# Two-layer gated network: the first layer's fourth batch in seven block products

## The chip, the cores and the metric

The kernel runs on one core of a Trainium2 chip. The core has a matrix engine (TensorE, PE in the profile), a vector engine (VectorE, DVE), a scalar engine (ScalarE, ACT), GpSimd (POOL), and SyncE (SP), which here only issues transfers. They run side by side, each through its own instructions in order, and wait for each other by semaphores. Matrix products are written to PSUM, everything else lies in SBUF, and DRAM is reached by DMA. The metric is the device time of one execution in microseconds, lower is better.

## The reference, cut to what matters

Two layers over x of shape (4, 512, 256). Each layer normalizes, computes a mixer `s` and a gate `g`, and adds their product to x. The gate is a feed-forward block with hidden width 1024, a Hadamard transform (`fwht`) of the hidden values and a down projection.

```python
def ffn(x, W1, W2, W3):
    hidden = silu(x @ W1.T) * (x @ W3.T)      # 256 -> 1024
    return fwht(hidden) @ W2.T                # 1024 -> 256

x = L0_attn_x
xn = layernorm(x)
s = L0_attn(xn)              # reduces to xn + rmsnorm(xn @ M) * norm_w
x = x + s * silu(ffn(xn, L0_ffn_W1, L0_ffn_W2, L0_ffn_W3))
xn = layernorm(x)
s = L1_attn(xn)              # causal attention with its own norm
x = x + s * silu(ffn(xn, L1_ffn_W1, L1_ffn_W2, L1_ffn_W3))
```

## The kernel before

Rows are tiled by 128. A batch has 512 rows (`NT` = 4 tiles of 128), the model width 256 is two blocks of 128, the hidden width 1024 eight blocks (`NH`). Each batch passes layer 0 first, all four of them (`f0_0` to `f0_3`; the profile leaves digits of names out, so `f_3gu` is the gate/up product of batch 3), then layer 1 (`f1_0` to `f1_3`).

**Numbers in two parts.** A value that enters a product is kept as a rounded part and the rest (`split`, L59: a cast on ScalarE, then a subtraction on VectorE). A product of two such values is three matmuls: high by high, high by low, low by high (`mm3`, L80).

**W2.** The Hadamard transform is moved into W2: `prep_w2` (L139) takes three steps of sums and differences on VectorE and a product with a 128 x 128 Hadamard matrix on TensorE, for each layer once. Layer 1's W2 is prepared beside batch 1 of layer 0 and stays in SBUF (`w2_tile`, L173, four buffers of 8 KB per partition under one tag).

**Layer 0** (`ffn`, L467). For each hidden block c, two gate/up products of 512 columns (six matmuls each), SiLU on ScalarE, multiplication on VectorE, a split, and the down product of the block before (twelve matmuls of 256 columns). All other work is given to a `Beside` object (L878) as a list of generators with a number of steps each; `slot` (L897) advances them evenly, twice per block. So program order is written by the slots, and from it a scheduler that simulates the engines makes the order of instructions of every engine. In `Beside` lie the gate of the batch before (`gate`, L691), the mixer (L714), the norm and transposition of the batch after (`norm`, L432), and preparations of weights.

**Layer 1** (`ffn_s`, L562). Here, for each quarter q of the hidden width, x (transposed) and the gate and up weights are each cut into 2 x 2 blocks, and their product is formed by Winograd's variant of Strassen's scheme from seven block products instead of eight. Each is six matmuls of 256 columns (`product`, L621). It needs sums of the weight blocks (`A11 ... S4`) and of x's blocks (`B11 ... T4`), and copies and additions between PSUM banks. There TensorE's order is fixed by hand (`line["fixed"]`): after each product, `place(n)` runs what the list `beside[q][n]` names. An integer there is a down product of the quarter before, a tuple one of an earlier quarter.

`prep_s` (L322) makes one quarter's weight sums: it loads four blocks (`sraw`, 512 KB), forms four sums on VectorE (`ssum`), splits the seven blocks (384 KB and 512 KB at a time) by a negated rounded copy and a rounded copy on ScalarE (`sp`), an accumulating transfer issued by GpSimd, which subtracts the rounded part, and stores both parts in DRAM. It is a generator of five steps. `load_s` (L350) brings a quarter back, two parts of 896 KB (`sw`), into two of four buffers, which the weights of layer 0 (`split_w13`, L118) hold before. The four quarters are prepared once, beside batches 2 and 3 of layer 0, and loaded again for every batch of layer 1.

`t_blocks` (L358) finds room for x's blocks: in W2's buffers for odd batches, in those of transposed xn (`xt_pair`, L304, two buffers) for even ones, and for batch 0 half of it in general scratch (`t4`, ten buffers of 4 KB per partition).

**Attention of layer 1.** `Attention` (L737): `xt` and `scaled` make the transposed, normalized and scaled input from the transposes `xt_half` (L744); `tq` and `v` are its first products. For batch 0 the transposes lie in `Beside` of `f0_3`, `tq` at the tail of `f0_3`, and `v` in the first quarter of `f1_0`.

Of the kernel before, what the change touches and what calls it, by code (L numbers as in the profile page):

```python
# [23 lines left out]
B = 4  # L24
# [11 lines left out]
def kernel(ctx: ExitStack, tc: tile.TileContext, a: dict, out: bass.AP):  # L36
# [101 lines left out]

    def prep_w2(layer, raws, dst, scratch):  # L139
# [3 lines left out]
        w2h, w2l = dst  # L143
        for half in range(2):
# [12 lines left out]
            if not native:  # L157
                bh = t4(f"w2bh_{layer}_{half}", [P, NH, P], F32R)
                bl = t4(f"w2bl_{layer}_{half}", [P, NH, P], F32R)
                split(cur, bh, bl)  # L160
                yield
# [11 lines left out]
    def w2_tile(name):  # L173
        return wp.tile([P, NH, D], F32R, tag="w2", name=name, bufs=4)

    def w2_tiles(layer):
        return w2_tile(f"w2h_{layer}"), w2_tile(f"w2l_{layer}")

# [125 lines left out]
    def xt_pair(name):  # L304

        both = act.tile([P, 2, 2, S], F32R, tag="xt", name=name, bufs=2)
        return both[:, 0], both[:, 1]
# [9 lines left out]

    A11, A12, A22, S1, S2, S3, S4 = range(7)
    B11, B22, B21, T1, T2, T3, T4 = range(7)
    sdram = {}  # L320

    def prep_s(q):  # L322

        raw = t4(f"sraw{q}", [P, 4, D])
        nc.sync.dma_start(raw, a["w13_1"][q])
        yield
        sums = t4(f"ssum{q}", [P, 4, D])
# [7 lines left out]
        sdram[q] = there = [  # L335
            dram.tile([P, 7, D], F32, tag=f"s{i}", name=f"s{i}_{q}", bufs=4) for i in range(2)
        ]

        for at, n, src in ((0, 3, raw), (3, 4, sums)):
            src = src[:, :n, :]  # L340
            hi, neg = (t4(f"sp{at}_{i}_{q}", [P, n, D], F32R) for i in range(2))
# [8 lines left out]
    def load_s(q, n):  # L350
        parts = [
            wp.tile([P, 7, D], F32R, tag="w13", name=f"sw{i}_{n}_{q}", bufs=4) for i in range(2)
        ]
        for i in range(2):
            nc.sync.dma_start(parts[i].bitcast(F32), sdram[q][i])
        return parts

    def t_blocks(b):  # L358

        if b % 2:  # L360
            whole = [w2_tile(f"tb{i}_{b}") for i in range(2)]
        else:
            whole = [
                act.tile([P, NH, D], F32R, tag="xt", name=f"tb{i}_{b}", bufs=2)
                for i in range(2 if b else 1)
            ]
        parts = [[w[:, i, :] for i in range(7)] for w in whole]
        if len(parts) < 2:
            lo3, lo4 = t4(f"tb3_{b}", [P, 3, D], F32R), t4(f"tb4_{b}", [P, 4, D], F32R)
            whole = [whole[0], None]  # L370
            parts.append([lo3[:, i, :] for i in range(3)] + [lo4[:, i, :] for i in range(4)])
            return parts, [(whole[0][:, 0, :], lo3[:, 0, :]),
                           (whole[0][:, 1:3, :], lo3[:, 1:3, :]),
                           (whole[0][:, 3:7, :], lo4)]
        return parts, [
            tuple(w[:, 0, :] for w in whole),
            tuple(w[:, 1:3, :] for w in whole),
            tuple(w[:, 3:7, :] for w in whole),
        ]

# [51 lines left out]
    def norm(layer, b):  # L432
# [5 lines left out]
        if layer:  # L438
# [18 lines left out]
            return  # L457
        hi, lo = xTs[0, b] = xt_pair(f"xt0_{b}")
# [8 lines left out]
    def ffn(name, xT, w13, w2, slot, defer=1, spare=(), parts=1, behind=False, tail=()):  # L467
# [86 lines left out]
        line["fixed"] = bool(tail)  # L554
        line["last"] = last_up
        for what in tail:
            what()
# [4 lines left out]
    def ffn_s(name, b, pairs, w2, beside, before, last=None):  # L562
# [4 lines left out]
        xh, xl = xTs[1, b]  # L567
# [40 lines left out]
        for q in range(NH // 2):  # L608
# [22 lines left out]
            copy = nc.vector.tensor_copy if q == 1 else nc.scalar.copy  # L631
# [45 lines left out]
            if q:  # L677
                left.pop()()
# [35 lines left out]
    def mixer(b):  # L714
# [5 lines left out]
        for i in range(2):  # L720
# [6 lines left out]
            yield  # L727
        nc.vector.tensor_scalar(r, r, 1.0 / D, RMS_EPS, ALU.mult, ALU.add)
# [6 lines left out]
        yield  # L735

    class Attention:  # L737
# [10 lines left out]
        def xt(self):  # L748
            b, mrb = self.b, mrs[self.b]
            xTs[1, b], (tb11, tb2x, tt) = t_blocks(b)  # L750
            self.xg = t4(f"xgh{b}", [P, 2, S], F32R), t4(f"xgl{b}", [P, 2, S], F32R)
            b1, b2 = self.halves
            early, late = slice(0, D), slice(D, S)
# [161 lines left out]
    NORM, MIXER, W2P = 3, 3, 12  # L915
# [80 lines left out]
    for b in range(B):  # L996
# [5 lines left out]
        if b:  # L1002
            tasks.append((call(gate_all, f"g0_{b - 1}", dn, xns[0, b - 1], xs[b - 1]), 1))
        tasks.append((mixer(b), MIXER))
        if b + 1 < B:
            if b:
                load_x(b + 1)
            if b == 2:
                tasks.append((prep_s(0), 5))
            tasks.append((norm(0, b + 1), NORM))  # L1010
        if b == 0:
            early = w2_tile("early0"), w2_tile("early1")
            spare = [
                [early[i][:, 2 * c : 2 * c + 2, :].rearrange("p a d -> p (a d)") for i in range(2)]
                for c in range(NH // 2)
            ]
        if b == 1:
            raw2_1 = load_w2(1)
            w2_1 = w2_tiles(1)
            tasks.append((prep_w2(1, raw2_1, w2_1, t4), W2P))  # L1020
            tasks.append((prep_second(), 5))
        if b == 2:
            tasks += [(prep_s(1), 5), (norm(1, 0), NORM), (prep_s(2), 5)]
        if b == 3:
            atts = [Attention(0)]
            at = atts[0]
            parts = run(at.xt_half, 0), run(at.xt_half, 1), at.xt, at.scaled, at.split_sums
            tasks += [(call(f), 1) for f in parts]
            norms = {1: norm(1, 1)}
            tasks.append((prep_s(3), 5))  # L1030
        bg = Beside(*tasks)
        if b == 0:
# [153 lines left out]
```

## Time and profile before

| | us |
|---|---|
| three runs | 364.04, 365.92, 366.18 |
| median | 365.92 |
| the profiled execution | 363.47 |
| its span in the profile | 361.3 |
| TensorE busy in it | 354.0 |
| VectorE, ScalarE busy | 278.5, 204.1 |

The span runs from the first to the last instruction; some 2.2 us of the profiled execution lie around it. An engine is busy while an instruction of it runs; matmuls overlap, so one shows about 284 ns where the next starts 118 ns later. In the answers by stretch, the numbers in brackets count instructions, the clock is the share of TensorE's full speed that was granted, and the DMA share is the mean over the core's 16 DMA engines.

The transfers that bear on the change, with their count, size and median time from issue to landing:

```profile
sw<-s SPq DMA_DIRECT2D x32, 896.0 KB, 5.1
...
sraw<-in_w SPq DMA_DIRECT2D x4, 512.0 KB, 3.6
s<-sp SPq DMA_DIRECT2D x4, 512.0 KB, 3.8
ssum<-sp POOLq DMA_DIRECT2D x4, 512.0 KB, 6.5
```

Each line is one group of transfers: destination and source, the queue that issues it, how many, how large, and how long until the data were there.

### The profile page before, as it was taken

The page shows a single profiled execution, that of the slowest core. Times are in us where ns is not written, and L with a number is a line of the kernel's source. Part 1 is how long each engine was busy: PE and PEld are TensorE (multiplying, and loading weights), DVE is VectorE, ACT ScalarE, POOL GpSimd, SP SyncE. Part 2 cuts the span into 40 slices and gives each one's busy share as a digit, 9 for nine tenths or more (in the row PEclk, how much of TensorE's full clock was granted, in tenths as well). Part 3 has the DMA queues.
Part 4 walks back from the last instruction along what each step waited for, and adds up shares of the span by engine and source line. Part 5 has one row for each costly group of instructions (what it writes and reads, how often), then busy time and mean ns, then how long its engine had stood idle before and what let it go on. Part 6 is the DMA issues. An engine that isn't in the chain of part 4 may idle for free.

```text
span 361.3 us, 6295 instructions
## 1 busy us (share of the span) xinstructions
PE 354.0 (98%) x2469; PEld 328.2 (91%) x2469; DVE 278.5 (77%) x584; ACT 204.1 (56%) x380; POOL 25.9 (7%) x30
## 2 busy tenths in 40 slices
PE   8999999999999999989999999999999999999995
PEld 6878998888988898868999999999999999999994
DVE  6897868996669835886986957989669897568645
ACT  4665436274494537764467655576655676446443
POOL 1000201100034101111100001100011000000000
PEclk9999999999999999999999999999999999999999
DMA  6935000301149626979356146572553645345401
GB/s 219 354 111 183 3 0 2 116 0 60 58 116 302 196 76 209 256 289 245 121 205 257 34 175 203 201 239 89 203 204 136 218 174 203 133 153 194 191 2 58
DMA packets 17436, 55.92 MB, mean 155 GB/s; under 512 B 1760, under 2 KB 8064, under 8 KB 17408
## 3 DMA queue, kind: packets, MB, share of 16 engines
q1 hardware_dynamic: 15968, 51.60, 39.7%
q0 software_dynamic: 1152, 3.67, 5.4%
q8 instruction: 19, 0.31, 0.3%
q10 hardware_dynamic: 288, 0.26, 0.2%
q14 instruction: 9, 0.07, 0.1%
HBM read 42.40 MB, written 9.45 MB: 144 GB/s over the span
## 4 chain that ended last, share of the span: by engine, by line
PE 78%; DVE 11%; DMA 6%; ACT 3%; issue 1%; POOL 1%; SPq 0%; DVEq 0%; ACTq 0%
PE f_0gu L70 6%; PE f_1gu L70 6%; PE f_2gu L70 6%; PE f_0dn L70 5%; PE f_2dn L70 5%; PE f_1dn L70 5%; PE f_3dn L70 4%; PE pv L70 4%; PE tq L70 3%; DMA sraw<-in_w 3%; PE o L70 2%; PE v L70 2%; DMA ssum<-sp 2%; PE sc L70 2%; PE f_3gu L70 2%; PE warm L70 2%
## 5 line engine op out<-in xcount | busy, mean ns | idle before, releaser
L70 PE MATMUL f_0gu<-xt,w 128*128 128x512 f32 (+1 forms) x108 | 24.8, 382 | 0.0
L70 PE MATMUL f_1gu<-xt,w 128*128 128x512 f32 x96 | 24.8, 395 | 0.0
L70 PE MATMUL f_3gu<-xt,w 128*128 128x512 f32 x96 | 24.7, 397 | 0.1
L70 PE MATMUL f_2gu<-xt,w 128*128 128x512 f32 x96 | 24.7, 395 | 0.0
L70 PEld LDWEIGHTS f_0gu<-xt,w 128*128 128x128 f32 x108 | 18.5, 188 | 4.4 <-issue 0.7
L70 PEld LDWEIGHTS f_3gu<-xt,w 128*128 128x128 f32 x96 | 17.2, 188 | 3.5 <-DVE f_3h L529 0.3
L70 PEld LDWEIGHTS f_2gu<-xt,w 128*128 128x128 f32 x96 | 17.2, 188 | 3.2
L70 PEld LDWEIGHTS f_1gu<-xt,w 128*128 128x128 f32 x96 | 17.1, 188 | 3.2
L61 ACT CAST f_1hh<-f_1h 128x512 fp32r<-128x512 f32 x16 | 10.0, 622 | 16.7 <-DVE f_1h L529 13.6
L70 PE MATMUL f_3dn<-w2h,f_3hh 128*128 128x256 f32 x64 | 17.9, 284 | 1.1 <-ACT f_3hh L61 1.1
L70 PE MATMUL f_1dn<-w2l,f_1hh 128*128 128x256 f32 x64 | 17.8, 282 | 0.0
L70 PE MATMUL f_1dn<-w2h,f_1hh 128*128 128x256 f32 x64 | 17.7, 281 | 0.0
L70 PE MATMUL f_3dn<-w2l,f_3hh 128*128 128x256 f32 x64 | 17.7, 281 | 0.0
L70 PE MATMUL f_2dn<-w2l,f_2hh 128*128 128x256 f32 x64 | 17.7, 281 | 0.0
L70 PE MATMUL f_2dn<-w2h,f_2hh 128*128 128x256 f32 x64 | 17.7, 281 | 0.0
L70 PE MATMUL f_3dn<-w2h,f_3hl 128*128 128x256 f32 x64 | 17.2, 282 | 0.0
L70 PE MATMUL f_1dn<-w2h,f_1hl 128*128 128x256 f32 x64 | 17.1, 282 | 0.0
L61 ACT CAST f_2hh<-f_2h 128x512 fp32r<-128x512 f32 x16 | 9.9, 620 | 12.6 <-DVE f_2h L529 9.5
L70 PE MATMUL f_2dn<-w2h,f_2hl 128*128 128x256 f32 x64 | 16.9, 282 | 0.0
L62 DVE TENSOR_TENSOR f_3hl<-f_3h,f_3hh 128x512 fp32r<-128x512 f32 (+1 forms) x17 | 11.1, 656 | 5.1 <-ACT f_3hh L61 5.0
L61 ACT CAST f_3hh<-f_3h 128x512 fp32r<-128x512 f32 (+1 forms) x17 | 10.0, 593 | 8.3 <-DVE f_3h L529 4.2
L62 DVE TENSOR_TENSOR f_2hl<-f_2h,f_2hh 128x512 fp32r<-128x512 f32 x16 | 10.9, 683 | 4.5 <-ACT f_2hh L61 4.4
(482 smaller groups left out, 1147.9 us busy)
## 6 DMA issues: line engine op xcount, KB each, us to landing
sw<-s SPq DMA_DIRECT2D x32, 896.0 KB, 5.1
w2raw<-in_w SPq DMA_DIRECT2D x4, 512.0 KB, 6.1
sraw<-in_w SPq DMA_DIRECT2D x4, 512.0 KB, 3.6
s<-sp SPq DMA_DIRECT2D x4, 512.0 KB, 3.8
ssum<-sp POOLq DMA_DIRECT2D x4, 512.0 KB, 6.5
s<-ssum SPq DMA_DIRECT2D x4, 512.0 KB, 3.0
mrb<-there SPq DMA_DIRECT2D x4, 512.0 KB, 3.8
w13raw<-in_w SPq DMA_DIRECT2D x3, 512.0 KB, 7.1
```

What stands on the lines that cost most here:

```text
L61: h = nc.scalar.copy(hi, src)
L62: return h, engine.tensor_tensor(lo, src, hi.bitcast(F32), ALU.subtract)
L70: ins = call(*args, **kwargs)
```

## The change

Layer 0's batch 3 is computed by `ffn_s` too. For this, `prep_s` takes a layer and prepares four quarters of layer 0's weights besides layer 1's, so eight in all: two beside batch 1, four beside batch 2, and two in hand-set places of batch 3. `load_s` streams 20 quarters in one list. `norm` makes x's blocks for batch 3 (`blocks_0`), with an eighth block for the mixer, which reads blocks as well (`Mixer`). Batch 2's last down product is left to batch 3's first places, and the gates of batches 2 and 3 move into places. Layer 1's W2 is stored in DRAM before its Hadamard product; the halves come back in `f0_3` and `f1_0` and are finished in `f1_0`. Transposed xn, W2 and x's blocks share six buffers. The mixer, gate and norm compute what they did.

```diff
     def prep_w2(layer, raws, dst, scratch):
...
+                if dst is None:
+                    there = dram.tile([P, 2, NH, P], F32, tag="w2", name=f"w2d_{half}")
+                    for i, part in enumerate((bh, bl)):
+                        nc.sync.dma_start(there[:, i], part.bitcast(F32))
+                    w2_dram.append(there)
+                    yield
+                    continue
...
     def w2_tile(name):
-        return wp.tile([P, NH, D], F32R, tag="w2", name=name, bufs=4)
+        return wp.tile([P, NH, D], F32R, tag="blk", name=name, bufs=6)
...
+    def load_half_w2(q):
+        parts = []
+        for half in range(2):
+            parts.append(t4(f"w2st_{half}_{q}", [P, 2, NH // 2, P], F32R))
+            there = w2_dram[half][:, :, q * NH // 2 : (q + 1) * NH // 2, :]
+            nc.sync.dma_start(parts[-1].bitcast(F32), there)
+        return parts
+
+    def last_of_w2(dst, q, half, part):
+        o = psum(f"w2ps_1_{half}_{q}", [P, NH // 2, P])
+        qs, ds_ = slice(q * NH // 2, (q + 1) * NH // 2), slice(half * P, (half + 1) * P)
+        for i in range(2):
+            matmul(o, had, part[:, i], start=i == 0, stop=i == 1)
+        split(o, *(z[:, qs, ds_] for z in dst))
...
     def xt_pair(name):
-        both = act.tile([P, 2, 2, S], F32R, tag="xt", name=name, bufs=2)
+        both = w2_tile(name).rearrange("p (i k h) d -> p i k (h d)", i=2, k=2)
...
-    def prep_s(q):
+    def prep_s(layer, q):
...
+    streams = [(0, q) for q in range(4)] + [(1, q) for _ in range(B) for q in range(4)]
+    loaded = []
+
+    def load_s(n):
+        while len(loaded) < min(n + 1, len(streams)):
+            layer, q = streams[len(loaded)]
+            parts = [
+                wp.tile([P, 7, D], F32R, tag="w13", name=f"sw{i}_{len(loaded)}", bufs=4)
+                for i in range(2)
             ]
+            for i in range(2):
+                nc.sync.dma_start(parts[i].bitcast(F32), sdram[layer, q][i])
+            loaded.append(parts)
+
+    def pairs_from(base):
+        def one(q):
+            load_s(base + q + 1)
+            return loaded[base + q]
+        return one
...
+    def blocks_0(b, b1, b2):
+        xTs[0, b], (tb11, tb2x, tt, tb12) = t_blocks(f"tb0_{b}_")
+        sums = t4(f"tsum0_{b}", [P, 4, D])
+        t1, t2_, t3, t4_ = (sums[:, i, :] for i in range(4))
+        b12 = t2(f"b12_0_{b}", [P, D])
+        nc.scalar.copy(b12, b1[:, early])
+        nc.vector.tensor_tensor(t1, b12, b1[:, late], ALU.subtract)
+        split(b1[:, late], *tb11)
+        nc.vector.tensor_tensor(t3, b2[:, early], b12, ALU.subtract)
+        nc.vector.tensor_tensor(t2_, b2[:, early], t1, ALU.subtract)
+        nc.vector.tensor_tensor(t4_, b2[:, late], t2_, ALU.subtract)
+        split(b2.rearrange("p (h n) -> p h n", h=2), *tb2x)
+        split(b12, *tb12)
+        split(sums, *tt)
...
+        if leave:
+            line["fixed"], line["last"] = True, last_up
+            return dn, [run(down, *queue[0], tiles) for tiles in ((0, 1), (2, 3))]
...
-            copy = nc.vector.tensor_copy if q == 1 else nc.scalar.copy
+            copy = nc.vector.tensor_copy if soft and q == 1 else nc.scalar.copy
...
         if b == 1:
+            tasks.append((prep_w2(1, load_w2(1), None, t4), W2P))
             tasks.append((prep_second(), 5))
+            tasks += [(prep_s(0, q), SUMS) for q in range(2)]
+            dn = ffn("f0_1", xTs[0, 1], w13, w2, Beside(*tasks).slot)
+            continue
+        tasks += [
+            (norm(1, 0), NORM), (prep_s(0, 2), SUMS), (prep_s(0, 3), SUMS), (prep_s(1, 0), SUMS),
+            (call(load_s, 0), 1), (prep_s(1, 1), SUMS), (call(load_s, 1), 1),
+        ]
+        dn, behind = ffn("f0_2", xTs[0, 2], w13, w2, Beside(*tasks).slot, leave=True)
...
+    p2, p3 = prep_s(1, 2), prep_s(1, 3)
+    norms = {1: norm(1, 1)}
+    places = [
+        [[0], [1, *steps(p2)], [silus[0]], [o[0], silus[1]], [], [o[1]], steps(p2), []],
+        [[o[2]], [o[3], *steps(p2)], [], [0, *steps(p3)], [adds[0]], [1, adds[1]], [2, *steps(p2)], steps(p3)],
+        [
+            [(0, 1, (2, 3))], [run(at.xt_half, 0), run(at.xt_half, 1), at.xt], [], [0, *steps(p2)],
+            [at.scaled], [1], [2, at.split_sums], steps(p3),
+        ],
+        [
+            [tq[0]], [tq[1]], [(1, 1, (2, 3))], [v_[0], *steps(p3)], [0], [v_[1]],
+            [1, lambda: w2_half.extend(load_half_w2(0))], [2, 3, *steps(p3), *steps(norms[1])],
+        ],
+    ]
+    behind, dn = ffn_s(
+        "f0_3", xTs[0, B - 1], pairs_from(0), w2, places, behind, soft=False
+    )
...
-            places = [[[v[0]], [v[1]], [v[2]], [sc[0]], [], [sc[1]], [v[3]], []]]
+        places = [[[v[2]], [v[3]], [0], [sc[0]], [1, silus[0]], [sc[1]], [2], [3, silus[1]]]]
+        if b == 0:
+            places[0][2].append(w2_last(0, 0))
+            places[0][4].append(w2_last(0, 1))
...
+            if b == 0:
+                places[1][3].append(lambda: w2_half.__setitem__(slice(2), load_half_w2(1)))
+                for half in range(2):
+                    places[2][6 + half].append(w2_last(1, half))
```

## The prediction

> **What bounds the kernel now.** I read the page's shares first, then stretches of the span one by one, then the order of time where TensorE (PE) idles, and last the waits of the DMA queue.
>
> ```profile
> span 361.3 us, 6295 instructions
> PE 354.0 (98%) x2469; PEld 328.2 (91%) x2469; DVE 278.5 (77%) x584; ACT 204.1 (56%) x380; POOL 25.9 (7%) x30
> ...
> DMA  6935000301149626979356146572553645345401
> ```
>
> PE is busy in all but 7.3 us of 361.3, and about 4 of those lie at the end, when the matmuls are done. So only two things pay: fewer matmuls, or a PE wait that goes. The DMA row says where transfers crowd: slices 12 and 16 to 18 stand at 7 to 9 tenths, between 108 and 171 us, just where the change adds traffic.
>
> The stretches are layer 0 batch 1, batch 2, batch 3, then layer 1 batch 0 and 1 (microseconds, busy time per engine, clock, DMA share, GB/s):
>
> ```profile
> 51.60:94.00 42.40, 42.40 (x260) 37.58 (x259) 35.39 (x63) 21.62 (x41) 2.76 (x2) 1.00 0.15 50
> 94.00:131.30 37.30, 37.30 (x221) 32.77 (x220) 27.52 (x73) 21.20 (x40) 7.91 (x8) 1.00 0.52 149
> 131.30:173.20 41.90, 40.77 (x245) 35.62 (x244) 29.34 (x62) 25.37 (x46) 5.60 (x6) 1.00 0.81 243
> 173.20:218.00 44.80, 44.64 (x358) 43.27 (x357) 36.38 (x73) 27.14 (x52) 1.01 (x1) 1.00 0.39 150
> 218.00:265.00 47.00, 46.89 (x375) 45.61 (x375) 39.40 (x87) 28.67 (x54) 2.32 (x2) 1.00 0.51 180
> ```
>
> Columns after the length are PE, weight loads, VectorE (DVE), ScalarE (ACT), GpSimd (POOL). The third row is the batch that changes: PE idles 1.1 us there, nowhere else in layer 0's later batches. The fourth and fifth show that a hand-ordered seven-product batch loses only 0.1 to 0.2 us, with DVE busy 81 to 84% and ACT 61%. In order of time, the 1.1 us:
>
> ```profile
> 157.69 1.68 PE L70 MATMUL f_3gu<-xt,w 128*128 128x512 f32 x6
> 157.78 0.85 ACT L342 ACTIVATE sp<-sraw 128x768 fp32r<-128x768 f32 x1 [1.63 <-DMA sraw<-in_w]
> ...
> 159.77 0.61 ACT L61 CAST f_3hh<-f_3h 128x512 fp32r<-128x512 f32 x1
> ...
> 160.44 0.38 PE L70 MATMUL f_3dn<-w2h,f_3hh 128*128 128x256 f32 x1 [1.08 <-ACT f_3hh L61]
> ```
>
> ACT waited 1.63 us for a transfer of block weights; the cast that PE needed stood behind it in ACT's queue, so PE stopped. One late transfer of a preparation (`prep_s`) reaches PE this way.
>
> **The change part by part.**
>
> *Products.* Out go 96 gate/up matmuls of 512 columns, in come 7 x 4 x 6 = 168 of 256. In the chain of waits 12 of `f_1gu` take 2.80 us (233 ns each), and 6 of `f_3gu1g` 0.71 (118 ns). 96 x 0.233 = 22.4; 168 x 0.1183 = 19.9: 2.5 us less PE. A rule speaks against it: the Trainium skill, "TensorE: Matmul & The Clock Gate", section "Back-to-back issue gap", gives sustained spacings of 81 ns at 128 columns and 131 ns at 512, so small matmuls cost more per column. Interpolated to 256 that is about 98 ns (estimate), and the sum would be 168 x 0.098 - 96 x 0.131 = +3.9 us. The trace has both shapes at a granted clock of 1.00, 233 and 118 ns, nearly proportional: I take -2.5.
>
> *The old wait.* The preparation that caused it is no longer there at that point; if nothing takes its place, -1.1. What is late next there is the same kind of wait at other points (below).
>
> *The start of batch 3.* Batch 2's last down product (12 matmuls, c = 7) is left for the first two places of the new order, after one product of 0.71 us. Ahead of it lie the down product of c = 6 (1.42) and that product: 2.1 us. What it needs after its last gate/up matmul: multiply 0.69, cast 0.62, subtract 0.69, the first two before the first matmul. Bounds 0 and 1.5 (one background operation of 1 us ahead on ACT); I take +0.5.
>
> *DVE and ACT in batch 3.* Per quarter q the seven-product form adds two DVE operations of 512 elements and three ACT copies (all on ACT here): DVE 8 x 0.6 = +5, ACT 12 x 0.5 = +6 (0.6 and 0.5 are the starts' spacing in runs of 0.69 and 0.59 us operations). Two of the four `v` tiles move in: 0.6 each. So DVE about 35 and ACT about 32 of a stretch of some 39 us, 90% and 82%, above any stretch that now runs without waits. Worst is q = 2: transposes, their block sums (3.6 us DVE), `scaled` (2.4) and the quarter's own 3.6 make 9.6 us of DVE between the last transpose and `tq`, over 7.1 us of PE. Layer 1's same quarter has 11.3 over 8.9 and shows no wait of `tq`: the excess, 2.4, is the same, but here DVE enters with the mixer's and the gates' work of q = 1 (1.7 us too much for that quarter). Bounds 0 and 3.5; I take +1.2.
>
> *DVE and ACT in batches 1 and 2.* A preparation is DVE 4 x 0.42, ACT 0.85 + 0.82 + 1.06 + 1.03 = 3.8, POOL two issues of 0.9. Batch 1 gets two (DVE +3.4, ACT +7.5), and loses four splits of W2 (0.66 and 0.6 each). Batch 2 has four instead of two, and blocks of batch 3's xn instead of two plain splits (DVE +3): DVE 34 of 37, ACT 30. PE covers that if the order is good: batch 1 has run at 83% DVE with no wait. 0, with bounds 0 and +3.
>
> *W2.* Its eight 512-column Hadamard matmuls leave batch 1 and return in layer 1 batch 0: PE zero. Four 512 KB stores go out where the DMA share is 0.15: hidden. They return as four 512 KB loads; four splits (DVE +2.4) join a batch with DVE at 36.4 of 44.8. Hidden; bounds 0 and 1. The one set of six buffers has the bytes of the two sets before; block tiles wait for xn and W2 to be released, which the order puts earlier. 0.
>
> *Queues.* SP issues some 36 more transfers of 0.32 us each; that is no time, but its stores wait for accumulating transfers, and pair loads stand behind them. POOL gets eight more issues; behind one that waits for ACT stands a `pow` (1.03 us) for a norm, for which DVE waits.
>
> *Transfers.* This is the unknown. A preparation moves 0.52 MB in, 0.92 accumulating, 2 x 0.92 out:
>
> ```profile
> 104.00:110.00 6.00, 6.00 (x31) 4.95 (x30) 5.63 (x13) 4.21 (x8) 2.20 (x3) 1.00 0.93 250
> 110.00:116.00 6.00, 6.00 (x36) 5.27 (x36) 5.37 (x23) 3.54 (x6) 2.65 (x3) 1.00 1.00 308
> 116.00:122.00 6.00, 6.00 (x39) 5.41 (x38) 6.00 (x18) 2.86 (x6) 1.36 (x2) 1.00 1.04 259
> 122.00:128.00 6.00, 6.00 (x36) 5.21 (x35) 3.22 (x10) 1.67 (x3) 1.03 (x1) 1.00 0.26 103
> ...
> 182.00:188.00 6.00, 6.00 (x46) 5.64 (x44) 5.06 (x11) 3.92 (x9) 0.00 (x0) 1.00 0.76 293
> ```
>
> Two preparations without their loads fill the engines for 6 x (0.93 + 1.00 + 1.04 + 0.26) = 19.4 us, 9.7 each; with the load (0.52 MB at the last row's 293/0.76 = 385 GB/s, 1.4) 11.1 us. A pair of block weights (1.84 MB) is 4.8. From 94 us to layer 1 at about 170 the new order wants six preparations (67), five pairs (24), half of W2, one x and one row broadcast (2.1 MB, 5): 96 us in 76. By the Trainium skill, "DMA: Bandwidth & Descriptors", section "Specifications", a core's HBM limit is about 358 GB/s; 31 MB would be 87 us (estimate). I keep the trace's 96, since it includes the accumulating transfers. By need it fits: three of the six (33 us) are for pairs that layer 1 reads 9 us or more after its start, 63 of 76. In queue order it doesn't, and runs 20 us over. So the cost lies between 0 and +20. The nearest row is batch 3 of before, at share 0.81, where one wait of 1.1 us came of it: in the main case I take none beyond the +1.2.
>
> Sum: -2.5 - 1.1 + 0.5 + 1.2 = -1.9. The profiled execution took 363.47 (span 361.3 and 2.2 around it): 361.6. The median, 365.92, lies 2.4 above that execution, so 364.0 as a median.
>
> **The rivals.** *Transfers bind (0.33).* Preparations run at 11 us each, so those of batch 2 run on into batch 3; ACT's in-order operations wait for their loads and buffers, and pair 1, due 7.9 us after batch 3 begins, or pairs 2 to 4, 8.5 us apart and more, land late. For it: 96 us in 76, and the 1.1 us wait at share 0.81. Against: layer 1's batch 0 has 27 us of DMA to spare, and the late three aren't due. It decides as soon as a pair lands over 8 us after its buffers come free. Half of the overrun, 10 us, on 364.0: 374.
>
> *DVE or ACT becomes the bound (0.19).* At 90% DVE in batches 2 and 3 the upper bounds of those terms hold in part: +3.5 over the main case, 367.5. For: the shares; against: layer 1's order at 84%.
>
> *It doesn't do what it says (0.04).* The scheduled batches before it fall out otherwise and eat the gain: 366.
>
> The main case, 364.0, has 0.44 and its own range is 362 to 365.5.
>
> **How the numbers follow.** From no change this kernel's measurement tells about 1% (3.66 us): 362.3 and 369.6. Faster than that: a quarter of the main case, 0.11. Slower: the transfer case and a little of the second, 0.34. Within: 0.55. The range 361.8 to 376 leaves out some 0.06 below and 0.14 above.
>
> **What would show it.** Gate/up matmuls of batch 3: 168 of 256 columns, near 20 us. Right: batch 3 about 39 us with PE idle under 2, batch 2 still idle-free, pair loads landing before their first product. Wrong: PE waiting on `sw` loads, or on ACT casts with `sraw`, `sp` or a staging tile ahead in ACT's queue; DMA share at 1 from 100 to 180 us. A batch 2 longer than 37.5 us, or a first quarter of layer 1 that waits for W2, would break the terms set to nothing.

## The result and the profile after

The changed kernel takes 413.48 us (412.15 to 414.29, four runs) against 364.98 for the kernel before in the same comparison: 1.1326 times as long, with an interval of 1.1269 to 1.1382. The forecast was 364.0 with a range up to 376. The profiled execution has a span of 412.5 us, 51.2 more than before.

The page after, its shares and its slices of 10.3 us:

```profile
span 412.5 us, 6611 instructions
PE 359.8 (87%) x2541; PEld 336.7 (82%) x2541; DVE 291.2 (71%) x614; ACT 226.8 (55%) x411; POOL 34.0 (8%) x38
...
PE   7999999999999641264199999999999999999994
...
PEclk9999999999999895558589999999999999999999
DMA  8733002779825899999988582346643472446401
```

There is one hole. In slices 14 to 20 (counted from 1), from 134 to 206 us, PE is busy at 1 to 6 tenths, the DMA row stands at 8 and 9, and the granted clock falls to 5 tenths. Outside the hole the PE row looks like that of the old kernel. From the start of each stage (first matmul, us):

| stage | before | after | two preparations only (e3, below) |
|---|---|---|---|
| layer 0, batch 3 | 128.3 | 125.8 | 126.1 |
| layer 1, batch 0 | 173.2 | 218.9 | 169.6 |
| layer 1, batch 1 | 218.6 | 268.7 | 218.1 |
| end of span | 361.3 | 412.5 | 360.9 |

Batch 3 took 93 us instead of 45, and it starts 2.5 earlier. Layer 1's batch 0 is 4.4 longer (W2's Hadamard products and some down products moved there), and what follows it 1.1. By stretch, with the columns as in the prediction (length, PE, weight loads, VectorE, ScalarE, GpSimd, clock, DMA share, GB/s):

```profile
94.00:130.00 36.00, 36.00 (x228) 32.27 (x227) 27.44 (x71) 16.72 (x36) 5.40 (x5) 1.00 0.67 213
130.00:170.00 40.00, 20.16 (x132) 18.58 (x131) 14.34 (x28) 18.53 (x27) 5.22 (x6) 0.76 0.92 279
170.00:210.00 40.00, 15.95 (x79) 14.33 (x80) 18.99 (x38) 22.44 (x38) 5.36 (x6) 0.60 1.00 308
```

No engine is busy for even 60% of 130 to 210 us; only the DMA engines are full. What PE waited for, over the whole kernel (engine, tile, what ended the wait: us in total, times, longest):

```profile
PE tq L70 <- ACT xgh L61: 14.6, 2, 10.5
PE f_3gu2g L70 <- DMA sw<-s: 13.1, 2, 7.8
PE xt_0tp L70 <- ACT osb L817: 12.3, 1, 12.3
```

These three carry 40 us of the 51.2. One is a pair of block weights (`sw`) that came late: it is quarter 2's, whose weights the third preparation makes. The other two name ScalarE, and a wait that names an engine asks what that engine stood behind. For `xt_0tp`, in order of time with the idle time before an instruction in brackets:

```profile
175.29 0.84 ACT L368 ACTIVATE sp<-sraw 128x768 fp32r<-128x768 f32 x1 [9.65 <-DMA sraw<-in_w]
...
177.86 1.03 ACT L369 CAST sp<-ssum 128x1024 fp32r<-128x1024 f32 x1
178.79 1.06 ACT L817 COPY osb<-o 128x512 f32<-128x512 f32 x2
...
179.42 1.12 PE L70 MATMUL xt_0tp<-ident,xn 128*128 128x128 f32 x4 [12.31 <-ACT osb L817]
```

ScalarE waited 9.65 us for the blocks of a preparation (`sraw`); the copy of the mixer's product, for which the transposes waited, stood behind it in line. It is the wait of 1.1 us of the old kernel, eleven times as long. The second wait of `tq`, 4.18 us, is of the same kind: two operations of a preparation, the second of which waits 1.29 us for a store, stand ahead of the cast that PE needs. (The first, 10.45 us, was not followed further.)

```profile
201.70 0.83 ACT L368 ACTIVATE sp<-sraw 128x768 fp32r<-128x768 f32 x1
203.82 0.83 ACT L369 CAST sp<-sraw 128x768 fp32r<-128x768 f32 x1 [1.29 <-DMA s<-ssum]
204.56 0.61 ACT L61 CAST xgh<-xg 128x512 fp32r<-128x512 f32 x1
...
205.22 0.80 PE L70 MATMUL tq<-xgh,wqkh 128*128 128x512 f32 x1 [4.18 <-ACT xgh L61]
```

Why the blocks were late is told by the chain of waits (start, length, what):

```profile
126.73 7.11 DMA sraw<-in_w
...
145.81 13.08 DMA sraw<-in_w
...
161.73 13.46 DMA sraw<-in_w
```

and by SP's queue, which issues these loads:

```profile
125.04 0.34 SPq L389 DMA_DIRECT2D sw<-s  x1
126.36 0.32 SPq L498 DMA_DIRECT2D mrb<-there  x1
126.73 0.43 SPq L351 DMA_DIRECT2D sraw<-in_w  x1
```

The third of the eight preparations, meant for batch 2, has its load issued only when batch 3 has begun: ahead of it in SP's line stood the second part of pair 1, for which a weight buffer of batch 2 had to come free, and the row broadcast of a norm. From 110 to 130 us the DMA share was only 0.39. Then six preparations ran one after the other, the loads issued at 126.7, 135.9, 145.8, 161.7, 177.7 and 186.4, each behind the stores of those before it. The groups of transfers show what that made of each:

```profile
sw<-s SPq DMA_DIRECT2D x40, 896.0 KB, 6.0
sraw<-in_w SPq DMA_DIRECT2D x8, 512.0 KB, 7.0
s<-sp SPq DMA_DIRECT2D x8, 512.0 KB, 13.0
ssum<-sp POOLq DMA_DIRECT2D x8, 512.0 KB, 9.5
```

A load of 512 KB lands after 7.0 us (median) instead of 3.6, a store after 13.0 instead of 3.8.

### The profile page after: what moved, and what is told of

It is laid out like the page before. It is cut to its first block, busy times and chain, and to the rows that moved or that the text cites. A ratio compares the mean times of both kernels' runs of the same rounds, so it can differ in the third digit from the quotient of the medians.

```text
span 412.5 us, 6611 instructions
## 1 busy us (share of the span) xinstructions
PE 359.8 (87%) x2541; PEld 336.7 (82%) x2541; DVE 291.2 (71%) x614; ACT 226.8 (55%) x411; POOL 34.0 (8%) x38
## 3 DMA queue, kind: packets, MB, share of 16 engines
q1 hardware_dynamic: 21664, 72.57, 48.8%
q0 software_dynamic: 2304, 7.34, 9.5%
## 4 chain that ended last, share of the span: by engine, by line
PE 65%; DMA 17%; DVE 11%; ACT 3%; issue 1%; SPq 1%; POOL 0%; DVEq 0%; ACTq 0%
DMA sraw<-in_w 9%; PE f_0gu L70 5%; PE f_1gu L70 5%; PE f_2gu L70 5%; PE f_0dn L70 4%; PE f_1dn L70 4%; PE f_2dn L70 4%; PE f_3dn L70 4%; PE pv L70 3%; DMA s<-ssum 3%; PE tq L70 3%; PE o L70 2%; PE sc L70 2%; DMA ssum<-sp 2%; DMA w2st<-w2d 1%; PE v L70 1%
## 5 line engine op out<-in xcount | busy, mean ns | idle before, releaser
L356 DVE TENSOR_TENSOR ssum<-sraw 128x256 f32<-128x256 f32 x8 | 3.4, 420 | 25.9 <-DMA sraw<-in_w 25.9
L70 PE MATMUL f_3gu2g<-tb,sw 128*128 128x256 f32 x48 | 8.7, 322 | 13.1 <-DMA sw<-s 13.1
L70 PE MATMUL tq<-xgh,wqkh 128*128 128x512 f32 x16 | 6.4, 473 | 14.6 <-ACT xgh L61 14.6
L368 ACT ACTIVATE sp<-sraw 128x768 fp32r<-128x768 f32 x8 | 6.7, 843 | 21.9 <-DMA sraw<-in_w 21.9
L70 PEld LDWEIGHTS f_3gu2g<-tb,sw 128*128 128x128 f32 x48 | 7.5, 223 | 13.6 <-DMA sw<-s 8.1
L70 PE MATMUL f_3dn<-w2l,f_3hh 128*128 128x256 f32 x64 | 18.6, 290 | 0.0
L70 PE MATMUL f_3dn<-w2h,f_3hl 128*128 128x256 f32 x64 | 18.5, 290 | 0.0
L61 ACT CAST f_2hh<-f_2h 128x512 fp32r<-128x512 f32 x16 | 10.0, 622 | 15.5 <-DVE f_2h L583 12.4
```

Of the source, the lines that this page charges most:

```text
L61: h = nc.scalar.copy(hi, src)
L70: ins = call(*args, **kwargs)
L356: nc.vector.tensor_tensor(s1, a21, a22, ALU.add)
L368: nc.scalar.mul(neg, src, -1.0)
```

## The experiments

The expectations call the experiments e1 to e16; their names stand beside the times here. Three theories stood at first. A: the six further preparations' transfers are too many for the stretch. B: the order on SP's queue, which leaves the DMA engines idle before the hole, is the whole of it. C: the seven-product batch itself, with its hand-set order and more VectorE and ScalarE work, loses the time. In e13 to e15 the letters change: B there is the preparations' own ScalarE and VectorE work, which holds PE in line whatever the bytes, and C that full DMA engines cost little unless somebody waits in line for a late transfer.

Runs of the kernel before taken beside these had medians of 363.5 to 364.4 us, single ones 363.4 to 366.9. Where an interval is given, the time is a median of four or more executions, as it is for e10 and e12; the others are one execution each, so only differences of several us are read from them.

### The new batch without the new preparations

Only the two preparations of batch 1 are left, and every pair is loaded from their results:

```diff
-                nc.sync.dma_start(parts[i].bitcast(F32), sdram[layer, q][i])
+                nc.sync.dma_start(parts[i].bitcast(F32), sdram[0, q % 2][i])
...
-            (norm(1, 0), NORM), (prep_s(0, 2), SUMS), (prep_s(0, 3), SUMS), (prep_s(1, 0), SUMS),
-            (call(load_s, 0), 1), (prep_s(1, 1), SUMS), (call(load_s, 1), 1),
+            (norm(1, 0), NORM), (call(load_s, 0), 1), (call(load_s, 1), 1),
...
-    p2, p3 = prep_s(1, 2), prep_s(1, 3)
+    p2, p3 = nothing(), nothing()
```

> The changed kernel with only the two preparations beside batch 1; all pairs are loaded from these two, so the output is another. From 94 us to layer 1 the engines then have five pairs and 5 us of others, 29 us of 76. Theories A and B: batch 3 runs in 39 us with little idle time of TensorE; 361 to 363, and 2 to 3 us below the old kernel with two preparations (e4), which is the products' 2.5. Theory C: VectorE at about 33 and ScalarE at 24 of 39 us still hold TensorE by several us, so no less than e4, 364 or more.

(e3) It took 362.51 us, ratio 0.9938 (0.9921 to 0.9954). For a fair partner, the old kernel with two preparations:

```diff
-            tasks += [(prep_s(1), 5), (norm(1, 0), NORM), (prep_s(2), 5)]
+            tasks += [(prep_s(1), 5), (norm(1, 0), NORM)]
...
-            tasks.append((prep_s(3), 5))
```

> The old kernel with only two preparations, both beside batch 2, from which all pairs are loaded; the output of layer 1 is another. The counterpart of e3. The one wait of 1.1 us that a late load caused goes: 364, against 365 with all four.

(e4) It took 361.69, ratio 0.9906 (0.987 to 0.9942). So the whole rest of the change, W2 in DRAM, shared buffers, hand-set order and 168 small products for 96 large ones, costs 0.8 us. C falls as the cause of 48 us: without the six preparations, the seven-product batch loses nothing of that size. But the change's own gain is also not there: by the spacing of the matmuls the products give the 2.5 us, and batch 3's own gaps take 3.5 (in order of time 0.38 at the first down product, 0.56, 0.35 and 0.76 at gate/up products, 1.48 at `tq`).

Are those gaps the work that moved in? The gates' additions and the mixer's last part were moved to the fourth quarter:

```diff
-        [[o[2]], [o[3], *steps(p2)], [], [0, *steps(p3)], [adds[0]], [1, adds[1]], [2, *steps(p2)], steps(p3)],
+        [[o[2]], [o[3], *steps(p2)], [], [0, *steps(p3)], [], [1], [2, *steps(p2)], steps(p3)],
...
+            [tq[0]], [tq[1]], [(1, 1, (2, 3))], [v_[0], *steps(p3)], [0, adds[0]], [v_[1], adds[1]],
+            [1, lambda: w2_half.extend(load_half_w2(0))], [2, 3, mix.last, *steps(p3), *steps(norms[1])],
```

> e3 (only the two preparations of batch 1), with the gates' additions and the mixer's last part moved from batch 3's second quarter to its fourth. e3 saved 2.5 us of products and waited 3.5 us in batch 3, of which 1.5 before tq and 0.8 before the first product after the transposes. If VectorE's load of the second quarter (4.9 us of moved work) causes these, they shrink and 1.5 to 2.5 us come back: 360 to 361. If they come of the chain from the transposes to tq alone, no change: 362.5.

(e10) 362.48 us: nothing, and PE's waits in batch 3 are those of e3. The gaps are not the moved work's.

### The old kernel with the new preparations

```diff
-            tasks += [(prep_s(1), 5), (norm(1, 0), NORM), (prep_s(2), 5)]
+            tasks += [(prep_s(1), 5), (norm(1, 0), NORM)]
+            tasks += [(prep_s(q), 5) for q in (4, 5, 6, 7, 2)]
```

> The old kernel, eight products in batch 3, with four more preparations after norm(1,0) beside batches 2 and 3, whose results nobody reads. Theory A, DMA time: the two batches had 19 + 34 = 53 us of DMA time in 79 and get 44 more, 97 in 79, nearly the changed kernel's 96 in 76. If overfull transfers cost what they overrun, +18 and more: 383 to 400, without one seven-product matmul in layer 0. Theory C, the hand order and VectorE or ScalarE in batch 3: ScalarE 15 us and VectorE 7 more in two batches that had room; up to +5, 366 to 370.

(e5) 401.95 us, 2 above A's range and far from C's 366 to 370. Two of the changed kernel's three waits are there, though layer 0 has not one seven-product matmul:

```profile
PE xt_0tp L70 <- ACT osb L724: 15.4, 1, 15.4
PE tq L70 <- ACT xgh L61: 14.0, 2, 8.1
```

From 94 us to layer 1 this kernel takes 117.6 us at a DMA share of 0.83: 97.6 us of DMA time (share times length), as A counted (97), and 20 unused, where the kernel before takes 79.2.

### Fewer of them, and another order

Three of the eight left out, pairs of layer 1 loaded from the first of layer 1's:

```diff
-            (call(load_s, 0), 1), (prep_s(1, 1), SUMS), (call(load_s, 1), 1),
+            (call(load_s, 0), 1), (call(load_s, 1), 1),
...
-    p2, p3 = prep_s(1, 2), prep_s(1, 3)
+    p2, p3 = nothing(), nothing()
```

> The changed kernel without the preparations of layer 1's quarters 1 to 3: quarter 0's weights are used for all four, so the output of layer 1 is another. Three of the six late preparations go, 33 us of DMA time and 11 us of ScalarE, 4 us of VectorE. Theory A: batch 3 is shorter by the DMA time, 413 - 33 = 380. Theory B: the other three are still behind the row broadcast; about the same, 380 to 385. Theory C: VectorE's 4 us at most, about 409.

(e2) 387.17 us: 26 less for three preparations, 8.8 each, where A and B had 28 to 33. And all eight, with preparations ahead of the norms in batch 2's list:

```diff
+        if b == 2:
+            tasks.append((prep_s(0, 2), SUMS))
         tasks.append((norm(0, b + 1), NORM))
...
-            (norm(1, 0), NORM), (prep_s(0, 2), SUMS), (prep_s(0, 3), SUMS), (prep_s(1, 0), SUMS),
+            (prep_s(0, 3), SUMS), (prep_s(1, 0), SUMS), (norm(1, 0), NORM),
```

> Batch 2's list reordered: preparation (0,2) ahead of norm(0,3), and (0,3) and (1,0) ahead of norm(1,0); nothing is left out. Theory A, the transfers are too many for the time they are given and the queue order leaves the engines idle before that: with work from about 100 us on, six preparations of 11.1, five pairs of 4.8 and 5 of other transfers are 96 us and end near 196 instead of 217, so about 20 us come back: 393. Theory B, the order on SyncE's queue is the whole of it: all comes back, 362 to 366. Theory C, VectorE and ScalarE are the bound in batch 3: no change, about 413.

(e1) 399.55 us: 14 less than the change, between A's 393 and C's 413. B's 362 to 366 is missed, so the order is not the whole. In the changed kernel the stretch from 94 us to layer 1 is 125 us at a DMA share of 0.86, so 107.5 us of DMA time and 17.5 unused. With the new order it is 112 at 0.96: again 107.5, and 4.5 unused. So the order is worth the unused part; the 107.5 stay. (That time wanted and time unused add up to the length is bookkeeping; whether the DMA engines or the work in line hold PE is for the next runs.) With two preparations the same stretch has 76 us at 0.58, 44 of DMA time: a preparation is (107.5 - 44) / 6 = 10.6 us, near the prediction's 11.1.

### The transfers alone, and the work alone

Both in the new order, with the pairs loaded from the first two preparations, so that no pair waits for the results of the six. First without the accumulating transfers and stores of the six (their loads stay):

```diff
+            if (layer, q) in ((0, 0), (0, 1)):
+                nc.gpsimd.dma_start(src, neg.bitcast(F32), accum_op=ALU.add)
+                nc.sync.dma_start(there[0][:, at : at + n, :], hi.bitcast(F32))
             yield
+            if (layer, q) in ((0, 0), (0, 1)):
+                nc.sync.dma_start(there[1][:, at : at + n, :], src)
```

> The new order of the lists, and from the third preparation on no accumulating transfer and no store: six preparations keep their load from memory and all their VectorE and ScalarE work, every pair is loaded from the first two preparations (output not the reference's). Theory A: 363 to 367, the two-preparation kernel (362.5) and at most some us of crowded engines. Theory B (ScalarE and VectorE in line): 380 or more. Against the next kernel it parts the engines' work from the transfers.

Then with the transfers, and without the VectorE and ScalarE work:

```diff
+        if (layer, q) not in ((0, 0), (0, 1)):
...
+                nc.sync.dma_start(there[0][:, at : at + n, :], src)
+                nc.gpsimd.dma_start(src, zero[:, :n, :], accum_op=ALU.add)
+                yield
+                nc.sync.dma_start(there[1][:, at : at + n, :], src)
```

> The new order of the lists, and from the third preparation on the transfers alone: load, accumulating transfer (from a tile of zeros) and the four stores, with no VectorE and ScalarE work; every pair is loaded from the first two preparations, so nothing waits for the six by data, only for the engines and queues (output not the reference's; nine staging buffers instead of ten). Theory A in the form 'the DMA engines are full, and whatever else needs them waits': 385 to 400. Theory C (a full DMA alone costs little; the loss needs somebody who waits in line for a late transfer, ScalarE's copies or the pairs): 363 to 372. Theory B: 363 to 367.

The work with its loads (e14) took 378.48 us, the transfers alone (e15) 405.17: 16.0 and 42.7 above the two-preparation kernel, where both together, in this order, are 37.0 above. Both lie outside the ranges of the theories: e14 between A's 363 to 367 and B's 380, e15 above A's 385 to 400. The transfers are enough for a loss of the whole size. ScalarE's copies need not wait for them, and C's 363 to 372 is missed; but what C said of late transfers stays, since PE waited for data of W2 (21.1 us) and of pairs (12.5) in e15. The stretches of e15:

```profile
130.00:170.00 40.00, 30.36 (x205) 29.46 (x203) 19.45 (x35) 16.89 (x36) 7.21 (x8) 0.83 1.00 328
170.00:210.00 40.00, 19.02 (x133) 17.65 (x132) 16.90 (x41) 10.95 (x19) 4.63 (x5) 0.78 0.98 308
```

and the longest wait of PE in that kernel, with SP's queue just before it:

```profile
PE w2ps L70 <- DMA w2st<-w2d: 21.1, 1, 21.1
```

```profile
198.97 8.65 SPq L363 DMA_DIRECT2D s<-sraw  x3
207.71 1.42 SPq L194 DMA_DIRECT2D w2st<-w2d  x2
```

Nobody needed those stores, but the loads of W2's half stood behind them in SP's line and were issued at 207.7, 19 us after layer 1 began. In this kernel each accumulating transfer waits for the store of the same tile, which the original doesn't, so the line is longer than there; and 24 of the 42.7 us lie in layer 1's batch 0, which takes 72.2 us here, 49.8 in the changed kernel and 48.5 with two preparations. So e15 shows what the transfers can cost, not their part of the loss.

The kernel with the work and its loads, at one of its waits, ScalarE and then PE in order of time:

```profile
130.98 1.04 ACT L368 ACTIVATE sp<-ssum 128x1024 fp32r<-128x1024 f32 x1
131.93 1.03 ACT L369 CAST sp<-ssum 128x1024 fp32r<-128x1024 f32 x1
132.87 0.57 ACT L691 COPY f_3gu0l<-f_3gu0g 128x512 f32<-128x512 f32 x1
133.38 0.61 ACT L61 CAST f_2hh<-f_2h 128x512 fp32r<-128x512 f32 x1
```

```profile
134.04 0.38 PE L70 MATMUL f_2dn<-w2h,f_2hh 128*128 128x256 f32 x1 [1.54 <-ACT f_2hh L61]
```

Two background operations of 1 us stand ahead of the cast that PE waits for. PE's waits for ScalarE and VectorE sum to 13.1 us in that kernel, 3.8 the longest, against 3.1 in the two-preparation kernel, and its batches 2 and 3 are 4 and 11.6 us longer. The rest of the 16 us is in PE's busy time, 357.4 us against 351.5 for the same matmuls: after its waits PE was granted less than the full clock (0.87 from 130 to 170 us). The loads are late here too: ScalarE waits 9.1 us for `sraw`, VectorE 8.6.

### Fewer bytes

From the third preparation on, two of the seven blocks are accumulated and stored, in the change's order and in the new one; the pair loads take the other five from the first two preparations:

```diff
+            some = n if (layer, q) in ((0, 0), (0, 1)) else 1
+            nc.gpsimd.dma_start(src[:, :some, :], neg.bitcast(F32)[:, :some, :], accum_op=ALU.add)
+            nc.sync.dma_start(there[0][:, at : at + some, :], hi.bitcast(F32)[:, :some, :])
```

> The changed kernel with the same preparations in the same places and the same list, but from the third preparation on the accumulating transfer and the stores move one block of three or four, 2/7 of the bytes; the pair loads keep their bytes and take the other blocks from the first two preparations, so the output is another. A preparation then takes 1.4 + 9.7 x 2/7 = 4.2 us of DMA time instead of 11.1. Theory A, DMA time: 6 x 6.9 = 41 us less, 413 - 41 = 372. Theory B, the order of the queues and the number of in-order waits: they are all still there, 395 to 413.

> Two earlier edits together: preparation (0,2) ahead of the norm of batch 3 and (0,3), (1,0) ahead of the norm of layer 1's batch 0, and from the third preparation on only two of the seven block weights go through the accumulating transfer and to DRAM (the other five come, for the pair loads, from the first two preparations, so the output is not the reference's). With the new order alone the stretch from 94 us to layer 1 held 107.5 us of DMA time in 112; with fewer bytes alone 74.5 in 102, 27 of them unused because the third preparation was issued late. Theory A (DMA time of a stretch that otherwise takes 76 us, plus the time that the order leaves unused): 74.5 fits in 76, so 366 to 374. Theory B (ScalarE's and VectorE's part of the preparations, in line, holds PE whatever the bytes): 385 to 392.

390.2 us (e9) lies between the theories, and 389.44 (e13) in B's range: A's 366 to 374 is missed. Yet the DMA time fell as it was meant to. In e13 the stretch from 94 us to layer 1 is 102.2 us long at a share of 0.73, so 74.6 us of DMA time, which fits in 76, and 27.6 unused. Of the 37.0 us that the new order loses with all its bytes, 10.1 came back. So DMA time that doesn't fit isn't the whole cause: with time that fits, the preparations still cost 27 us. PE's waits in e13 name ScalarE and VectorE alone, 19.8 us, and those wait for `sraw` for 11.7 and 12.4 us; PE's busy time is 9.9 us longer than with two preparations. That is 11 us worse than e14, which has the same work; this difference was not taken apart. (Over the whole kernel the edit saves less DMA time than bytes: the pair loads, now in pieces, take packets of 1 to 3 KB, and SP's queue moves 64.72 MB in 37,216 packets in 195 us, where it moved 72.57 in 21,664 in 201.)

### GpSimd instead of the accumulating transfer

The subtraction moves to GpSimd. The negated copies go, and with them the accumulating transfers, 39 us of DMA time in all. It was tried in the change, in the new order, and in the kernel before.

```diff
-            hi, neg = (t4(f"sp{at}_{i}_{layer}_{q}", [P, n, D], F32R) for i in range(2))
-            nc.scalar.mul(neg, src, -1.0)
+            hi = t4(f"sp{at}_{layer}_{q}", [P, n, D], F32R)
             nc.scalar.copy(hi, src)
-            nc.gpsimd.dma_start(src, neg.bitcast(F32), accum_op=ALU.add)
+            nc.gpsimd.tensor_tensor(src, src, hi.bitcast(F32), ALU.subtract)
```

> The changed kernel, but in each preparation GpSimd subtracts the rounded part itself; the negated copy on ScalarE and the accumulating transfer go. The accumulating transfers are 4.9 us of DMA time in each preparation, the copies 1.9 us of ScalarE. Theory A: six preparations in batch 3 take 6.2 instead of 11.1, 29 us less: 413 - 29 = 384, less still if the chain through the transfer (7 to 10 us to land) was what held each preparation. Theory B: the queue order still holds them; 390 to 413. Theory C: 405 or more.

> As e6, with e1's order of batch 2's list. Theory A: 6 x 6.2 + 24 + 5 = 66 us of DMA time from 100 us to layer 1 at 170, so nearly all fits: 366 to 372, where what is left over e3 (362.5) is waits for single transfers. Theory B alone (order): e1's 399 less little.

> The old kernel with GpSimd's subtraction in its four preparations. e4 showed that two preparations fewer give 2.7 us. ScalarE loses 7.5 us and the DMA engines 20 in batches 2 and 3. If the late load was what TensorE waited for, 362 to 363.5; if GpSimd is slow at 768 and 1024 elements[...], 365 or more.

390.41 (e6); 383.34, ratio 1.0522 (1.0499 to 1.0546) (e7); and 362.61, ratio 0.9962 (0.9948 to 0.9976) (e8). It helps the change by 23 and the new order by 16 us and is no rescue: A's 384 for the first and 366 to 372 for the second are missed. On the kernel before it is a gain of 0.4%, and the only version of the whole computation here that beats both kernels.

### Spread over all batches

One preparation beside batch 0, three beside batch 1, three beside batch 2, one in batch 3; with GpSimd's subtraction, the same with the moves of the fourth quarter, and with the accumulating transfer:

```diff
+            tasks.append((prep_s(0, 0), SUMS))
...
+            tasks.append((prep_s(0, 1), SUMS))
             tasks.append((prep_w2(1, load_w2(1), None, t4), W2P))
+            tasks.append((prep_s(0, 2), SUMS))
             tasks.append((prep_second(), 5))
-            tasks += [(prep_s(0, q), SUMS) for q in range(2)]
+            tasks.append((prep_s(0, 3), SUMS))
```

> The changed kernel with GpSimd's subtraction and the preparations spread to where the DMA engines were idle: one beside batch 0, three beside batch 1 between the other tasks, three beside batch 2, one in batch 3. All are computed. Theory A: from 94 us about 4 x 6.2 + 24 + 5 = 54 us of DMA time for 76, so transfers no longer bind: 364 to 368, e3's 362.5 plus VectorE's 7 and ScalarE's 7 us of six preparations. Theory B or C: 375 or more.

> e11 with e10's later additions. 1.5 to 2.5 us below e11 if VectorE's load in the second quarter holds TensorE: 362 to 366. It beats the old kernel with GpSimd's subtraction (e8, 362.6) only at the lower end.

> One preparation beside batch 0, three beside batch 1, three beside batch 2, one in batch 3, as in the spread kernel of before, but with the accumulating transfer instead of GpSimd's subtraction (the spread kernel with GpSimd took 384.8). If GpSimd's subtractions beside VectorE were what the spread kernel lost (DVE at 10.0 of 10 us in 70-80 and 120-130 us, PE idle there): 366 to 376. If the DMA time decides (39 us more of it, some 125 us wanted between 60 and 180): 380 to 392. If VectorE's block sums themselves, put beside batches 1 and 2, decide: 380 to 388 with PE waiting for DVE in those batches and DMA share below 0.9.

384.82, ratio 1.0573 (1.0523 to 1.0623) (e11); 385.56 (e12); and 386.68 (e16). A's 364 to 368 for the first and the 362 to 366 for the second are missed. It is the same time by two ways. With GpSimd, the DMA share is 0.79 from 100 to 130 us and 0.71 from 130 to 190, and VectorE has no time left just where PE idles:

```profile
70.00:80.00 10.00, 8.06 (x38) 6.39 (x37) 10.00 (x16) 3.03 (x5) 0.41 (x1) 0.88 0.34 136
120.00:130.00 10.00, 8.21 (x49) 6.55 (x47) 10.00 (x26) 2.16 (x5) 3.45 (x2) 1.00 0.93 332
```

With the accumulating transfer the DMA engines are full again:

```profile
100.00:130.00 30.00, 28.31 (x176) 25.15 (x175) 27.17 (x75) 19.48 (x37) 8.01 (x8) 1.00 1.04 318
130.00:190.00 60.00, 44.51 (x298) 42.22 (x297) 33.54 (x61) 34.31 (x61) 6.29 (x7) 0.83 0.93 293
```

That falls in the range put down for DMA time. That VectorE's load makes the 22 us of the first is read from these rows, not shown by a run of its own.

## Why the prediction was wrong

The step that failed is *Transfers*: "in the main case I take none beyond the +1.2", with +20 as the upper bound. The six further preparations cost 51 us, as the runs without them show (e3 against the change). The rival *Transfers bind* named the way, ScalarE's in-order operations waiting for loads and late pairs, and its waits came as written; the DMA share of 1 came too (0.98), but from 134 to 206 us instead of 100 to 180. It had 0.33 of the chance and a price of 10 us. The price failed in four ways, and the clock came on top.

- *The sum.* 96 us of DMA time in 76 were counted; 107.5 were wanted. The price of a preparation was nearly right (10.6 measured). What was left out is the end of the first two, whose last store goes out at 103 us in the two-preparation kernel (share 1.02 from 94 to 109): the stretch already holds 44 us there, where the count had 29 for pairs, W2 and rows.
- *"By need it fits."* It was assumed that three preparations could run on into layer 1 at no cost. But by the change's own order their steps stand in batch 2's list and batch 3's places, so on ScalarE and VectorE they come before layer 1's work, and their loads and stores stand in one SP line with the pairs and W2's halves. All six ran inside batch 3; their last store went out at 217.1 us.
- *Queues.* "That is no time" holds for the issue of 0.32 us, not for what the line does: the third load went out at 126.7 us. Of the stretch's 17.5 us without DMA work, 11.4 lie before it, and the new order gave 14 us back. The overrun of 31.5 and the 17.5 are the 49 us by which the stretch from 94 us to layer 1 is longer than 76.
- *The work in line.* The preparations' ScalarE and VectorE operations were put at nothing (*DVE and ACT in batches 1 and 2*) and at +1.2 (*in batch 3*). With their loads, and with no accumulating transfer or store, they cost 16 us (e14), and with DMA time that fits, 27 (e13). How the 51 us divide between full DMA engines and work in line stays open: the two don't add up (42.7 and 16.0 apart, 37.0 together in the new order).
- *The clock.* PE was busy for 359.8 us against 351.5 in the two-preparation kernel, with the same 2541 matmuls. PE idled for much of 130 to 210 us and was granted 0.76 and 0.60 there, and 0.50 from 170 to 179 us, where it did nothing. The Trainium skill, "TensorE: Matmul & The Clock Gate", section "What's actually happening", says that an idle window of about 3.4 us halves the clock; the PEclk row's 5 agrees. How much of these 8.3 us the end felt wasn't measured; they lie in a stretch that is held up anyway.

The other steps: *Products*, -2.5: the 0.71 us for six small matmuls held in batch 3. *The start of batch 3*, +0.5: 0.38 in the two-preparation kernel. *The old wait*: gone where it was, and back eleven times as long. *W2*, 0: PE waited 0.9 us. *DVE and ACT in batch 3*, +1.2 with bounds 0 and 3.5: the other gaps of the two-preparation kernel sum to 3.15, near the upper bound, with `tq` the largest as said, though not for the moved work (e10). *DVE and ACT in batches 1 and 2*, 0 with an upper bound of 3: in the changed kernel the four preparations of batch 2 never ran in it, so its 35.9 us are those of the two-preparation kernel; where they do run there, without stores (e14), batch 2 is 4 us longer.

A second sum had pointed the same way. The limit of 358 GB/s that the Trainium skill gives in "DMA: Bandwidth & Descriptors", section "Specifications", made 87 us (estimate) of these transfers, and that too is over 76; plain transfers moved 360 GB/s of DMA time here (last section). Both sums said that it didn't fit; the argument about need talked them away.

## What to carry to other kernels

When a change adds transfers, add up DMA time for the stretch in which they must run, with all that earlier work still has under way, and do not count on a late part running on past the stretch before you have read where its steps stand in every engine's line. Read each queue's order: a load behind a store that waits for something is as late as that store (21.1 us of PE's time in e15), and an in-order engine hands the delay to whoever stands behind (12.3 us in the change). That the DMA time fits is not enough: in e13 it fitted, and the preparations still cost 27 us. A gain of 2.5 us in matmuls didn't pay here for four extra preparations of 10.6 us of DMA time and 3.8 us of ScalarE each.

## What the runs showed of the hardware

Queues of the kernel before, then of the one after (packets, MB, share of 16 engines' span); `q1` has SP's plain transfers, `q0` the accumulating ones:

```profile
q1 hardware_dynamic: 15968, 51.60, 39.7%
q0 software_dynamic: 1152, 3.67, 5.4%
```

```profile
q1 hardware_dynamic: 21664, 72.57, 48.8%
q0 software_dynamic: 2304, 7.34, 9.5%
```

DMA time is the share times the span. Plain transfers moved 51.60 MB in 143 us of it and 72.57 in 201, both 360 GB/s; accumulating ones 3.67 MB in 19.5 and 7.34 in 39.2, 188 and 187 GB/s. In these kernels an accumulated byte cost nearly twice the DMA time of a plain one.

GpSimd's subtraction of two tiles takes 2.1 us on average for 768 and 2.5 for 1024 elements per partition (1.85 and 2.36 the shortest), and a VectorE subtraction of two SBUF tiles is slower beside it. The kernel with GpSimd and the new order (e7), VectorE's split and then GpSimd's row:

```profile
162.96 2.07 DVE L62 TENSOR_TENSOR f_3hl<-f_3h,f_3hh 128x512 fp32r<-128x512 f32 x1 [0.69 <-ACT f_3hh L61]
...
166.31 0.69 DVE L62 TENSOR_TENSOR f_3hl<-f_3h,f_3hh 128x512 fp32r<-128x512 f32 x1 [0.68 <-ACT f_3hh L61]
```

```profile
161.68 2.80 POOL L369 TENSOR_TENSOR ssum<-ssum,sp 128x1024 f32<-128x1024 f32 x1
```

The split that begins while GpSimd works takes 2.07 us, the next one, with GpSimd idle, 0.69. The first ends 0.55 us after GpSimd's row does. Two other splits that begin beside a GpSimd subtraction, of 2.50 us in this kernel (at 94.32) and 2.76 in e8 (at 168.21), end 0.55 us after it too, as if they had stood until it was done.
